# A quarter of block 4's gates through ScalarE and GpSimd while the route runs

## The chip, the core and the metric

The kernel runs on one core of a Trainium2 chip. A core has five engines, each with its own queue of instructions, executed in order: TensorE (PE in the profile; PEld is its loading of weights), VectorE (DVE), ScalarE (ACT), GpSimd (POOL) and SyncE (SP, which here only issues DMAs). They meet through semaphores. TensorE writes its results to PSUM, a memory of eight banks of 128 x 512 float32 numbers; the others work between PSUM and SBUF, except that in this kernel GpSimd only works on SBUF. The metric is the time of one execution on the device, in microseconds, and less is better.

## What is computed

Four blocks run one after the other over 2048 tokens of width 128: two attention blocks with their feed-forward parts, a third attention block, and block 4, a mixture of 64 small experts. Only block 4 is touched:

```
router_scores = softmax(xt @ Wr + br)
fs = _grouped_routing_scores(router_scores)      # sort each expert's scores, groups of 64, keep the best
up = jnp.einsum('td,edh->teh', xt, Wup) + bup
gate = jnp.einsum('td,edh->teh', xt, Wgate) + bgate
h = silu(up) * gate * fs[:, :, None]
out = jnp.einsum('teh,ehd->td', h, Wdown) + fs @ bdown
```

The 64 experts have 32 hidden features each, so the ups are a matrix of 2048 features by 2048 tokens, and the gates another. The routing sorts the scores of every expert over its tokens and keeps the best groups; it needs no up and no gate, and these need no routing until the product with `fs`.

## The kernel before

**The route.** The function `route` is the backbone: sorting passes on VectorE (`sort_pass`: one max and one min per pass over two halves of an SBUF tile, L1504 and L1505), then a search for the threshold by five counts over 2048 numbers (L1875), then small instructions that exchange sums with TensorE (L1906 to L1942), a scan (L1958) and the mask. After it the rows are multiplied by the weights and TensorE does the down projection (`stage_d`).

**The experts.** Between these instructions the class `Experts` places the up and gate work. The 2048 x 2048 plane is cut into 32 units of 256 features by 512 tokens, each of two halves (128 x 512), so there are 64 halves. `up` issues one matmul on TensorE and a Silu with bias on ScalarE out of PSUM into the unit's rows `hid` (L1650). `feed` issues gate matmuls ahead and keeps three (four when the ups are used up) in the list `ready`; an up is issued first where its half still lacks it. `fill(n)` takes up to n of the waiting gates: for each, VectorE adds the bias and multiplies the PSUM tile into `hid` in one instruction (L1664), then one further up and one further gate matmul are issued. All up and gate matmuls stand on one line, L1641, in `matmul`. PSUM gives them four banks.

**The order.** `stage_d` runs under a manual schedule: on TensorE, ScalarE, VectorE and GpSimd the instructions keep the order in which the program writes them. A fill is written after one sorting pass or more, so VectorE's order is pass, pass, gate, pass, pass, gate. Near the end come `fill(3)` at L1861, L1894, L1909, L1927 and L1940, placed where VectorE would wait for TensorE, and `fill(64)` at L1957, which takes what is left.

**Other names.** `c_xn` is a tag of one SBUF buffer of 128 x 512 float32: block 3 uses it at its start, and `route` at its end for `r_chosen`. The halves of the sorted keys are exchanged by two DMAs (L1830 on SyncE, L1831 on ScalarE's queue) before L1837. GpSimd has two memsets in the route and just after it, L1956 and L1692. L1858 and L1859 transpose the group sums on TensorE and copy them on ScalarE for the first count.

Of the kernel before, what the change touches and what calls it, by code (L numbers as in the profile page):

```python
# [22 lines left out]
F32 = mybir.dt.float32  # L23
BF16 = mybir.dt.bfloat16
AF = mybir.ActivationFunctionType
ALU = mybir.AluOpType
AX = mybir.AxisListType

P = 128
# [481 lines left out]
def add_tiles(k, x, ps):  # L511

    k.nc.vector.tensor_tensor(x, x, ps.rearrange("p (i d) -> p i d", d=D), ALU.add)
# [498 lines left out]
class BlockC:  # L1012
# [391 lines left out]
    def gate(self, b, j):  # L1404

        k, nc, st = self.k, self.k.nc, self.st[b]
        at, n = self.GROUPS[j]
        local, remote = st["local", j][:, :n], st["remote", j][:, :n]
        gs = self.p2.tile([P, 2, 64], F32, tag="gs", name=k.name("gs"))
        g = gs[:, 0, : n * 16]  # L1410
        l3 = local.rearrange("p m (h d) -> p (m h) d", d=8)
        pws = []
        last = (b, j) == (NB - 1, 2)
        eng = nc.vector if last else nc.gpsimd

        def products():
            for a, wn in ((local, "c_gl"), (remote, "c_gr")):
                pw = self.p2.tile([P, 64, 8], F32, tag="pw", name=k.name("pw"))[:, : n * 16]
                eng.tensor_tensor(
                    pw, a.rearrange("p m (h d) -> p (m h) d", d=8),  # L1420
                    k.row(wn)[:, None, :].to_broadcast([P, n * 16, 8]), ALU.mult,
                )
                pws.append(pw)
            if not last:
                eng.tensor_tensor(local, local, remote, ALU.subtract)

        def sums():
            for i in range(2):
                nc.vector.tensor_reduce(gs[:, i, : n * 16], pws[i], AX.X, ALU.add)
            nc.vector.tensor_tensor(g, g, gs[:, 1, : n * 16], ALU.add)  # L1430
            if last:
                tanh()
                eng.tensor_tensor(local, local, remote, ALU.subtract)

        def tanh():
            nc.scalar.activation(g, g, AF.Tanh, scale=0.5)

        def mix():
            if not last:
                tanh()  # L1440
            eng.tensor_scalar(g, g, 0.5, 0.5, ALU.mult, ALU.add)
            eng.tensor_tensor(l3, l3, g[:, :, None].to_broadcast([P, n * 16, 8]), ALU.mult)
            eng.tensor_tensor(local, local, remote, ALU.add)

        mT = self.p1.tile([P, 512], F32, tag="mT", name=k.name("mT"))

        def features():
            ps = k.mm()
            for i in range(n):
                nc.tensor.transpose(ps[:, i * P : (i + 1) * P], local[:, i, :], k.ident)  # L1450
            nc.scalar.copy(mT[:, : n * P], ps[:, : n * P])

        def out():
            ps = k.mm()
            for i in range(n):
                nc.tensor.matmul(
                    ps[:, i * D : (i + 1) * D], mT[:, i * P : (i + 1) * P], k.c_out,
                    start=True, stop=True,
                )
            add_tiles(k, k.xo[:, b * MT + at : b * MT + at + n], ps[:, : n * D])  # L1460
            self.front.tiles(self.pipe, b, at, n)

        beats = (0, 0, 1, 1, 1) if last else (1, 2, 1, 3, 2)
        steps = ((False, products), (False, sums), (False, mix), (True, features), (True, out))
        if last:
            products()
            sums()
            beats, steps = beats[2:], steps[2:]
        self.pipe.chain(*((n, *step) for n, step in zip(beats, steps)))
# [134 lines left out]
class Experts:  # L1604
# [50 lines left out]
    def feed(self):  # L1655

        while self.gates and len(self.ready) < (3 if self.ups else 4):
            unit, e = self.gates.pop(0)
            while (unit, e) in self.ups:
                self.up()  # L1660
            ps, hd = self.matmul(unit, e, self.k.d_gate), self.hid[unit][:, e, :]
            bias = self.k.col("d_bgate", unit[2] + 8 * e)
            self.ready.append(
                lambda ps=ps, hd=hd, bias=bias: self.k.nc.vector.scalar_tensor_tensor(  # L1664
                    hd, ps, bias, hd, ALU.add, ALU.mult
                )
            )

    def fill(self, n=1):

        for _ in range(n):
            if self.ready:
                self.ready.pop(0)()
                self.up()
                self.feed()


def stage_d(k, out, front, ex):
# [104 lines left out]


def route(k, p1, front, fill):


# [23 lines left out]
    for n, f in enumerate(front.todo):  # L1811
        f()
        left = len(front.todo) - n
        if left in (24, 13, 11):
            next(first)
        elif left == 6:
            next(second)
        fill(n % 2 if left < 10 else n % 3 > 0)
# [6 lines left out]
    while j >= 1:  # L1825
        sort_pass(k, za, zb, 1024, j, j == 512)
        fill()
        za, zb = zb, za
        j //= 2
# [384 lines left out]
```

## Time and profile before

| what | value |
|---|---|
| median of 3 runs | 1298.76 us (1298.31 to 1298.89) |
| profiled execution | 1301.14 us, of which the span of instructions is 1299.4 us |
| mean granted TensorE clock | 0.963 |
| busy: PE, PEld, DVE, ACT, POOL | 1155.7, 741.2, 869.4, 645.1, 477.8 us |
| L1664, gates on VectorE | 64 instructions, 747 ns each, 1085.3 to 1205.2 us |
| L1650, Silu on ScalarE | 64 instructions, 686 ns each |
| L1641, ups and gates on TensorE | 256 records (two for a matmul), 1052.9 to 1204.3 us |
| VectorE's waits for L1641 ahead of L1664 | 5.9 us in 7 waits |
| GpSimd in 1085 to 1205 us | two memsets, 1.09 us |

How to read it: the span runs from the first to the last instruction of one profiled execution, and the runs without a profile are the ones that the median is taken from. Busy shares are averages over stages with very different limits, so for a change in one stage the rows of that stage count: its busy times, its waits, and the chain of work that ended last, followed back from the last instruction. A row of a timeline has the start, the duration, the engine, the line, the operation, what it writes and reads, and in brackets how long the engine was idle ahead of it and who released it.

### The profile page before, as it was taken

How to read it: one execution, taken by the hardware profiler on the slowest of the kernel's cores; microseconds unless marked ns; L12 is line 12 of the kernel's file. 1: busy time of each engine (PE TensorE's matmuls, PEld its weight loads, DVE VectorE, ACT ScalarE, POOL GpSimd, SP SyncE). 2: the span in 40 equal slices, each digit the busy share in tenths (PEclk: the TensorE clock that was granted, in tenths of full speed). 3: DMA queues.
4: the chain of work that ended last, by engine and by line, in shares of the span. 5: the costliest groups of instructions: out<-in, count | busy, mean ns of one | idle time of the engine just before them, and what ended most of it. 6: DMA issues, size and time to landing. Idle time of an engine off the chain costs nothing.

```text
span 1299.4 us, 23474 instructions
## 1 busy us (share of the span) xinstructions
PE 1155.7 (89%) x9441; PEld 741.2 (57%) x9441; DVE 869.4 (67%) x1794; ACT 645.1 (50%) x1212; POOL 477.8 (37%) x556
## 2 busy tenths in 40 slices
PE   5899999998588999999999787989999967898798
PEld 3566666665356666666656544655555532343698
DVE  5566666565477776776776535566568969998763
ACT  5455455454345665665665545666756743342000
POOL 1523333232488776676686342221231210000000
PEclk9899999999799999999999988989988988999899
DMA  9000000000010000010100030000000000000000
GB/s 294 2 1 1 1 1 1 2 1 1 17 26 22 23 22 18 22 26 18 26 22 18 5 109 9 1 2 2 1 2 1 2 1 1 0 17 0 25 17 17
DMA packets 19841, 25.18 MB, mean 19 GB/s; under 512 B 2762, under 2 KB 13716, under 8 KB 19476
## 3 DMA queue, kind: packets, MB, share of 16 engines
q1 hardware_dynamic: 19076, 23.02, 6.3%
q8 instruction: 75, 1.23, 0.4%
q10 hardware_dynamic: 656, 0.66, 0.2%
q14 instruction: 34, 0.28, 0.1%
HBM read 13.32 MB, written 1.05 MB: 11 GB/s over the span
## 4 chain that ended last, share of the span: by engine, by line
PE 43%; DVE 19%; ACT 7%; issue 3%; POOL 2%; DVEq 0%; POOLq 0%; ACTq 0%
PE big L1641 6%; PE mm L1716 5%; PE bank L947 4%; PE s L714 3%; PE s L822 3%; PE s L1250 2%; PE bank L867 2%; PE s L1246 2%; PE tr L1287 2%; DVE nm L1255 2%; PE bank L964 2%; DVE rinv L736 2%; DVE rinv L737 1%; PE mm L1298 1%; PE s L817 1%
## 5 line engine op out<-in xcount | busy, mean ns | idle before, releaser
L1255 DVE TENSOR_REDUCE nm<-s 128x4 f32<-128x1024 f32 (+1 forms) x64 | 71.0, 1152 | 59.9 <-PE s L1250 59.7
L761 POOL TENSOR_TENSOR t<-raw,tab 128x512 f32<-128x512 f32 x64 | 79.7, 1265 | 77.7 <-DVE raw L752 77.7
L377 DVE TENSOR_REDUCE nm<-s 128x1 f32<-128x1024 f32 x64 | 75.1, 1216 | 48.7 <-PE s L371 48.7
L1288 ACT COPY pT<-tr 128x512 f32<-128x512 f32 x120 | 70.0, 597 | 73.0 <-PE tr L1287 72.8
L1650 ACT ACTIVATE hid<-big,cols 128x512 f32<-128x512 f32 x62 | 41.9, 686 | 75.8 <-PE big L1641 75.7
L1287 PE MATMUL tr<-ident,pr 128*128 128x128 f32 x480 | 77.2, 284 | 2.6 <-ACT pT L1288 2.3
L768 POOL TENSOR_TENSOR raw<-raw,tab 128x1024 f32<-128x1024 f32 x32 | 75.4, 2358 | 2.4
L1641 PE MATMUL big<-xTd,d_gate 128*128 128x512 f32 x128 | 66.1, 610 | 11.2 <-ACT hid L1650 7.5
L723 ACT ACTIVATE sq<-s 128x1024 f32<-128x1024 f32 x32 | 32.8, 1024 | 85.7 <-PE s L714 85.7
L1641 PE MATMUL big<-xTd,d_up 128*128 128x512 f32 x128 | 70.5, 642 | 5.3 <-DVE hid L1664 3.2
L383 ACT ACTIVATE pr<-s,nm 128x1024 f32<-128x1024 f32 x64 | 71.0, 1120 | 8.3 <-DVE nm L377 8.2
L775 POOL TENSOR_TENSOR raw<-raw,t 128x1024 f32<-128x1024 f32 x31 | 73.2, 2361 | 1.7
L394 PEld LDWEIGHTS bank<-ident,pr 128*128 128x128 f32 x512 | 56.6, 142 | 30.0 <-issue 22.5
L406 PE MATMUL bank<-pT,v 128*64 128x128 f32 x1024 | 71.0, 282 | 0.7 <-DVE pT L399 0.2
L397 ACT COPY pT<-bank 128x512 f32<-128x512 f32 x64 | 34.9, 587 | 68.7 <-PE bank L394 68.7
L406 PEld LDWEIGHTS bank<-pT,v 128*64 128x64 f32 x1024 | 55.8, 138 | 22.5 <-issue 11.1
L1287 PEld LDWEIGHTS tr<-ident,pr 128*128 128x128 f32 x480 | 54.7, 144 | 21.0 <-issue 11.6
L371 PE MATMUL s<-kk,q 64*128 64x512 f32 x256 | 65.1, 619 | 0.6 <-ACT pr L383 0.5
L394 PE MATMUL bank<-ident,pr 128*128 128x128 f32 x512 | 65.7, 277 | 0.0
L714 PE MATMUL s<-b_wqkv,hT 128*128 128x512 f32 x128 | 64.0, 623 | 1.3 <-ACT hT L682 1.3
L1716 PEld LDWEIGHTS mm<-d_down,hid 128*128 128x128 f32 x496 | 60.4, 194 | 5.7 <-DVE xo L1747 1.9
L1716 PE MATMUL mm<-d_down,hid 128*128 128x128 f32 x496 | 61.1, 278 | 1.3 <-DVE xo L1747 1.3
(363 smaller groups left out, 2816.6 us busy)
## 6 DMA issues: line engine op xcount, KB each, us to landing
vs<-v SPq DMA_DIRECT2D x60, 130.0 KB, 2.2
b_wqkv<-in_L_ffn_wqkv_dram SPq DMA_DIRECT2D x2, 768.0 KB, 9.3
b_tab<-in_c_xpos_dram SPq DMA_DIRECT2D x1, 1024.0 KB, 8.0
d_up<-in_L_ffn_Wup_dram SPq DMA_DIRECT2D x1, 1024.0 KB, 5.4
d_gate<-in_L_ffn_Wgate_dram SPq DMA_DIRECT2D x1, 1024.0 KB, 7.3
out_dram<-xo SPq DMA_DIRECT2D x3, 256.0 KB, 2.3
rows<-in_rows_dram SPq DMA_DIRECT2D x1, 760.0 KB, 6.5
b_w<-in_L_ffn_w_dram SPq DMA_DIRECT2D x2, 341.0 KB, 8.1
```

The source lines that it names most:

```text
L377: nc.vector.tensor_reduce(t["nm"][h], t["s"][h], AX.X, ALU.max, negate=True)
L383: nc.scalar.activation(t["pr", h], t["s"][h], AF.Exp, bias=t["nm"][h], accum_out=st["sums"][:, h, qt % 4 : qt % 4 + 1],)
L394: nc.tensor.transpose(ps[:, i * P : (i + 1) * P], t["pr", h][:, at : at + P], k.ident)
L406: nc.tensor.matmul(t["u"][h * 64 : h * 64 + 64, :P], v[:, kb, h * 64 : h * 64 + 64], t["pT"][:, h, kb], start=(kb == 0), stop=(kb == MT - 1),)
L714: nc.tensor.matmul(qk[:, cut], lhsT, k.b_wqkv[:, l, cut], start=True, stop=True)
L761: nc.gpsimd.tensor_tensor(t2[:, :, :, a : a + 32], r4[:, :, :, z : z + 32], self.tabs[l][1][:, m, :, None, a : a + 32].to_broadcast([P, 2, ...
L768: nc.gpsimd.tensor_tensor(r4, r4, self.tabs[l][0][:, m, :, None, :].to_broadcast([P, 2, 8, 64]), ALU.mult)
L775: eng.tensor_tensor(flat, flat, t["t2"].rearrange("p j h d -> p (j h d)"), ALU.add)
L1255: nc.vector.tensor_reduce(nm[h], view[h], AX.X, ALU.max, negate=True)
L1287: nc.tensor.transpose(ps[:, c * P : (c + 1) * P], pr[:, c, t * P : (t + 1) * P], k.ident)
L1641: self.k.nc.tensor.matmul(ps, weights[:, rows], self.xT[:, cut], start=True, stop=True)
L1716: nc.tensor.matmul(sums[part][:, cols], hid[tp, h, c][:, e, cols], k.d_down[:, c + 8 * e, :], start=start and e == 0, stop=False,)
```

## The change

In `feed` the entry of `ready` becomes a tuple with a flag. The flag is set where, after the half is taken from the list, the number of gates left gives 1 modulo 4. In `fill` a flagged half goes to ScalarE, which writes gate plus bias to a temporary in SBUF (tag `c_xn`), and GpSimd multiplies the temporary into `hid`; the others go to VectorE as before. A flagged half does not count against n.

```diff
             ps, hd = self.matmul(unit, e, self.k.d_gate), self.hid[unit][:, e, :]
             bias = self.k.col("d_bgate", unit[2] + 8 * e)
-            self.ready.append(
-                lambda ps=ps, hd=hd, bias=bias: self.k.nc.vector.scalar_tensor_tensor(
-                    hd, ps, bias, hd, ALU.add, ALU.mult
-                )
-            )
+            self.ready.append((len(self.gates) % 4 == 1, ps, hd, bias))
+
+    def gate(self, aside, ps, hd, bias):
+        nc, k = self.k.nc, self.k
+        if aside:
+            t = k.wpool.tile([P, 512], F32, tag="c_xn", name=k.name("aside"))
+            nc.scalar.activation(t, ps, AF.Identity, bias=bias)
+            nc.gpsimd.tensor_tensor(hd, hd, t, ALU.mult)
+        else:
+            nc.vector.scalar_tensor_tensor(hd, ps, bias, hd, ALU.add, ALU.mult)
 
     def fill(self, n=1):
 
-        for _ in range(n):
-            if self.ready:
-                self.ready.pop(0)()
-                self.up()
-                self.feed()
+
+        while n and self.ready:
+            now = self.ready.pop(0)
+            self.gate(*now)
+            self.up()
+            self.feed()
+            n -= not now[0]
```

## The prediction

> **What bounds the kernel now.** I began with the busy times of each engine in stretches of the route (sort and selection of block 4, 1085 to 1205 us of the span), where all changed instructions run. Each engine's column is busy us and the number of instructions.
>
> ```profile
> 1125.00:1142.00 17.00, 16.22 (x35) 5.85 (x36) 17.00 (x29) 5.50 (x8) 0.00 (x0) 1.00 0.00 0
> 1142.00:1161.00 19.00, 18.71 (x55) 8.44 (x54) 18.38 (x27) 9.22 (x15) 0.00 (x0) 1.00 0.13 28
> 1161.00:1180.00 19.00, 14.80 (x34) 5.52 (x32) 18.14 (x42) 6.32 (x10) 1.09 (x2) 1.00 0.00 0
> ```
>
> The order is TensorE matmul, its weight loads, VectorE, ScalarE, GpSimd. VectorE is full (17.00 of 17), ScalarE a third to half busy, GpSimd empty. But TensorE is nearly full beside it (18.71 of 19). Then the chain of waits:
>
> ```profile
> 1126.72 32.17 PE big L1641 x70
> ...
> 1176.19 2.35 DVE r_zab L1875 x2
> 1178.55 0.66 DVE hid L1664
> ```
>
> For 32 us it runs through the matmuls of L1641, and only then through VectorE. The two are level: relief of VectorE pays until TensorE is the later one. Third, TensorE's matmuls in order of time (a float32 matmul is two records, so each row is one half's up or gate):
>
> ```profile
> 1129.48 1.13 PE L1641 MATMUL big<-xTd,d_up 128*128 128x512 f32 x2
> 1130.44 1.02 PE L1641 MATMUL big<-xTd,d_gate 128*128 128x512 f32 x2
> 1131.38 1.13 PE L1641 MATMUL big<-xTd,d_up 128*128 128x512 f32 x2
> ...
> 1149.10 1.02 PE L1641 MATMUL big<-xTd,d_gate 128*128 128x512 f32 x2
> 1149.96 1.02 PE L1641 MATMUL big<-xTd,d_up 128*128 128x512 f32 x2
> 1150.82 1.02 PE L1641 MATMUL big<-xTd,d_gate 128*128 128x512 f32 x2
> ```
>
> At its fastest a matmul starts each 0.858 us (1149.10, 1149.96, 1150.82), so an up and a gate, a pair, take 1.715 us. Around 1130 a pair takes 1.90: the up waits until the Silu before it has freed its PSUM bank.
>
> **What the change does, in counts.** The condition picks halves 2, 6, ... 62 (counted from 0): 16 of 64. A fill now pays its n in VectorE gates and does passing halves on top. So 48 VectorE gates remain, the same fills are met in the same order, and the gates are used up at the 48th, the first of the fill(3) at L1909 (1182.52 us now). Up to there each fill brings 4/3 of a pair.
>
> **Part 1, what VectorE loses.** A gate takes 747 ns, but the next instruction starts 0.66 us after its start, so 16 gates are 10.6 us. They all go at the end: after gate 48 (1183.2) the fills are empty until the scan L1958 (1205.20). Those 22.0 us are 16 gates (10.6), waits of 5.6 like the one below, and 5.8 of the selection's own small instructions.
>
> ```profile
> 1183.97 0.75 DVE L1664 SCALAR_TENSOR_TENSOR hid<-big,cols,hid 128x512 f32<-128x512 f32 x1 [0.71 <-PE big L1641]
> ```
>
> What is late next are the hand-overs to TensorE at L1906, L1926 and L1936, which the gates cover now: a small matmul takes about 0.3 us and each hand-over 0.05 to 0.1, some 0.9 together with what gate 48 and L1938 still cover. The stretch becomes 5.8 + 0.9 = 6.7: **-15.3 us**.
>
> **Part 2, what TensorE must do earlier.** VectorE gate 39, the last before the first big count L1875 (1161.85), is now half 51. From 1086.11, when halves 0 to 3 have their gates and the ups are ahead, TensorE must issue 48 gates and 48 ups: 96 x 0.858 = 82.4; its first two start slow (1.87 and 1.52 instead of 0.86): +1.7; the 16 transposes of L1858 stand before half 51 in its order: +2.3. That is 1172.5; with the matmul's tail 0.16, the gate 0.66 and two small instructions 0.35, L1875 starts at 1173.7: **+11.8 us**, if TensorE never stops. It did stop between 1086 and 1159: 70 calls are 61.7 us with the slow start, of 72.6. Most of these 10.9 us are gaps behind VectorE, which the denser order fills; for those early on, while three halves are waiting and TensorE may not run ahead, I keep **+2** (bounds 0 and 5). In the five rounds of L1875 (3.59 us each) 4/3 pair costs 2.3, so nothing is added.
>
> **Part 3, ScalarE.** The Identity with bias out of PSUM has a row, L1147, and its product on GpSimd has L316, of the same shape:
>
> ```profile
> L1147 ACT ACTIVATE qT<-mm,cols x4: 687/687/738, 766.0 to 842.5; 128x512 f32<-128x512 f32 x4
> L316 POOL TENSOR_TENSOR kk<-kt,a_rot x8: 1260/1272/1277, 18.6 to 227.1; 128x512 f32<-128x512 f32 x8
> ```
>
> 16 x 0.69 = 11 us lie in idle ScalarE time (1.0 to 1.2 us ahead of each Silu). Behind an Identity on ScalarE stand the next Silu, and behind that the next up; the half was computed three pairs before, so nothing waits. If that cover were gone, a Silu would be 0.69 late. No table load is added: L1147 ran between exponentials without one. But where the bank freed by ScalarE is reused at once a pair takes 1.90, as at 1130; half of 48 pairs x 0.185 is 4.4 (bounds 0 and 8.9), most of it inside stops already counted: **+1**.
>
> **Part 4, GpSimd.** 16 x 1.27 us on an idle engine; the temporary has one buffer, but a side half comes only each fourth. Behind the last product on its queue stand the memsets L1956 (0.95) and L1692; the scan that needs the first comes several us later. The half swap's DMA from ScalarE's queue (L1831) stands behind Silus as now, and the gates of the fills between cover its 3 us.
>
> Here a rule speaks against the change. The Trainium skill, GPSIMD Engine Reference, section Key points, says that GpSimd shares its SBUF interfaces with VectorE and contends with VectorE instructions that have two SBUF inputs. All sort passes have two; the gate itself, with PSUM as one input, has one. The rule has no price. The trace has, where products of block 3 meet early passes:
>
> ```profile
> 1039.99 0.79 POOL L1443 TENSOR_TENSOR local<-local,remote 128x256 f32<-128x256 f32 x1
> ...
> 1040.23 0.84 DVE L1504 TENSOR_TENSOR r_zab<-r_zab 128x256 f32<-128x256 f32 x1
> ...
> 1040.99 0.41 DVE L1505 TENSOR_TENSOR r_zab<-r_zab 128x256 f32<-128x256 f32 x1
> ```
>
> The pass that starts inside the product takes 0.84 instead of the 0.41 of its twin: it is held until GpSimd is done (1040.78) and ends 0.29 later. A pass already running is not disturbed. So a 1.27 us product holds VectorE by 1.27, less what is left of the running pass (0.2 to 0.3), less 0.14: about 0.85. Of 16 products 12 (halves 2 to 46) lie among passes: between 0 (all fall on gates and waits) and 12 x 0.98 = 11.8. The row gives 0.85, some fall on a gate: 8 us held. The first seven products come while VectorE is level with TensorE and delay both; later ones fall into VectorE's waits for gates. I count less than half: **+3.3**. Without the rule the sum would be lower by this.
>
> **Sum.** -15.3 + 11.8 + 2 + 1 + 3.3 = **+2.8 us**. The profiled execution took 1301.14 (span 1299.4 and 1.7 around it), so it would take 1303.9; on the median of the runs shown, 1298.76, it is **1301.6 us**. A measurement of this kernel can tell about 0.2% (2.6 us) from no change.
>
> **Rivals.**
> - TensorE keeps its fastest pace and the holds fall into waits. For it: 1.715 per pair held from 1146 to 1158 and wherever VectorE waits. Against it: the row of L1504. Then 11.8 - 15.3 = -3.5: **1295.3**, faster. It decides if stops, bank waits and holds together stay under 3.5. VectorE alone (-15.3 and no delay) would be 1283, which Part 2 excludes.
> - The holds stay uncovered: 8 and the early 2 on the path, +6.5 in sum: **1305.3**. For it: early on VectorE has no slack. Against: later it waits for gates.
> - Banks: each pair at 1.90, 8.9 us, with holds hidden beneath: +5.4 to +6.4, **1304.7**. For it: the gaps at 1130. Against: from 1146 they are gone as soon as VectorE waits.
> - The change doesn't do what it says, because nothing is set aside or a table is loaded for each Identity (32 x 1.28 = 41 us): the rows of L1147 exclude the latter.
>
> **Chances.** The forecast's own case, 1298.8 to 1304.3: 0.50; fast rival 0.21; holds 0.16; banks 0.12; the last 0.01. Faster by over 0.2% (under 1296.2) takes nearly all of the fast rival: 0.19. The forecast's case divides about its middle, just past 1301.4: with the two slow rivals slower is 0.53, the same 0.28. The range leaves out a tenth each side: from 1294.5 (the fast rival and a little of unseen gain) to 1307.
>
> **What would show it.** 48 rows of L1664, 16 of Identity near 0.69 us and 16 products near 1.27; the first L1875 some 15 to 18 us later than 1161.85, the scan L1958 some 1 to 5 us later than 1205.20; passes of L1504 and L1505 with maxima above 1 us and about 8 us held in sum; VectorE's waits for L1641 up from 5.9 to near 10 us, and before L1875 now. I am wrong if L1875 starts before 1172, if the passes keep their means (290, 430 and 685 ns), or if a pair takes over 1.9 us where VectorE waits.

## The result, and the profile after

The changed kernel took 1303.2 us (median of 20 runs, 1301.57 to 1306.76), the kernel before, beside it on the same chip, 1299.95 us (20 runs, 1298.31 to 1304.18). The ratio is 1.0027, 95% interval 1.0019 to 1.0034: 3.5 us slower (2.5 to 4.4). The forecast was 2.8 us slower.

The profiled execution took 1301.58 us, with a span of 1299.8. It came into the route earlier than the one of before: L1578, one VectorE pass ahead of the first gates and alike in all kernels here, starts at 1075.20 in place of 1078.69. Over all profiles of this study that point lies between 1075.20 and 1081.41, so every stretch below is counted from L1578 and not from the start of the span. Line numbers behind the change are 7 or 8 higher: the gate is L1672, Identity L1669, product L1670, the counts L1882, the scan L1965.

| stretch, us | before | after | difference | forecast |
|---|---|---|---|---|
| L1578 to the first count | 83.16 | 99.92 | +16.8 | +18.1 |
| first count to the scan | 43.35 | 29.50 | -13.9 | -15.3 |
| scan to the end of the span | 94.2 | 95.2 | +1.0 | 0 |

First the busy times by stretches of the route in the profile after, to be laid beside those of before (the columns are TensorE, its weight loads, VectorE, ScalarE, GpSimd, each busy us and instructions, then TensorE's granted clock):

```profile
1125.00:1142.00 17.00, 16.88 (x39) 6.97 (x38) 16.80 (x25) 7.78 (x12) 4.13 (x3) 1.00 0.01 1
1142.00:1161.00 19.00, 19.00 (x45) 8.36 (x44) 14.71 (x21) 9.87 (x17) 2.54 (x2) 1.00 0.13 28
1161.00:1180.00 19.00, 18.68 (x55) 8.78 (x54) 14.00 (x23) 10.69 (x18) 4.43 (x3) 1.00 0.00 0
1180.00:1205.00 25.00, 12.60 (x31) 5.51 (x29) 21.91 (x62) 1.47 (x3) 4.83 (x5) 0.76 0.00 1
```

The last of these stretches, from 1180 to 1205, looked like this in the kernel before:

```profile
1180.00:1205.00 25.00, 23.73 (x65) 11.08 (x64) 19.08 (x48) 5.50 (x8) 0.00 (x0) 1.00 0.00 1
```

TensorE has become the full engine before the counts (19.00 of 19), and VectorE, full before, now has nearly a quarter free (14.71 of 19). In the last stretch it is the other way round: TensorE works half of the time (12.60 of 25), and its clock falls to 0.76 on the mean, where it had been 1.00. The chain of waits of the same profile (start, us, what) says where one takes over from the other:

```profile
1125.14 1.64 DVE r_zab L1504
1126.77 0.60 DVE r_zab L1505
1127.38 0.67 DVE hid L1672
1128.09 41.76 PE big L1641 x96
1169.85 0.45 PE tr L1865 x4
...
1172.10 1.73 PE big L1641 x4
1173.93 0.75 DVE hid L1672
1175.12 2.35 DVE r_zab L1882 x2
```

Up to 1127 it is made of VectorE's own instructions, then of 96 records of TensorE without a break, the transposes, and the two matmuls of half 51, which stand behind them. The first count (the chain's last row) waits for that half's gate. VectorE's timeline has the same gate, with 4.01 us of idle time ahead of it, and another of the waits that it now has in the sort:

```profile
1151.08 0.75 DVE L1672 SCALAR_TENSOR_TENSOR hid<-big,cols,hid 128x512 f32<-128x512 f32 x1 [2.75 <-PE big L1641]
1173.93 0.75 DVE L1672 SCALAR_TENSOR_TENSOR hid<-big,cols,hid 128x512 f32<-128x512 f32 x1 [4.01 <-PE big L1641]
```

The added instructions (minimum, median and maximum in ns; the sixteenth product, of 1267 ns, has a row of its own, since the last rows of `hid` lie in another buffer), and a product among VectorE's passes in the timeline:

```profile
L1669 ACT ACTIVATE aside<-big,cols x16: 679/681/689, 1085.3 to 1196.0; 128x512 f32<-128x512 f32 x16
L1670 POOL TENSOR_TENSOR hid<-hid,aside x15: 1263/1270/1892, 1086.1 to 1184.6; 128x512 f32<-128x512 f32 x15
```

```profile
1094.49 1.27 POOL L1670 TENSOR_TENSOR hid<-hid,aside 128x512 f32<-128x512 f32 x1 [7.16 <-ACT aside L1669]
1094.60 1.31 DVE L1504 TENSOR_TENSOR r_zab<-r_zab 128x128 f32<-128x128 f32 x1
...
1095.83 0.28 DVE L1505 TENSOR_TENSOR r_zab<-r_zab 128x128 f32<-128x128 f32 x1
```

The pass of 128 numbers, 0.29 us as a rule, takes 1.31 and ends 0.15 after the product (1095.76). Eleven VectorE instructions are prolonged so, 8.25 us in all over what their line and shape take as a rule: ten in the sort and one small instruction of the count rounds. In the kernel before none is. No gate of L1672 is among them, and none of the long counts L1882, which read one tensor from SBUF.

### The profile page after: what moved, and what is told of

It is laid out like the page before. It is cut to its first block, busy times and chain, and to the rows that moved or that the text cites. A ratio compares the mean times of both kernels' runs of the same rounds, so it can differ in the third digit from the quotient of the medians.

```text
span 1299.8 us, 23422 instructions
## 1 busy us (share of the span) xinstructions
PE 1144.8 (88%) x9381; PEld 744.6 (57%) x9441; DVE 866.8 (67%) x1778; ACT 655.3 (50%) x1228; POOL 501.0 (39%) x572
## 3 DMA queue, kind: packets, MB, share of 16 engines
HBM read 13.32 MB, written 1.05 MB: 11 GB/s over the span
## 4 chain that ended last, share of the span: by engine, by line
PE 40%; DVE 20%; ACT 7%; issue 4%; POOL 3%; DVEq 0%; POOLq 0%; ACTq 0%
PE mm L1723 5%; PE big L1641 4%; PE bank L947 4%; PE s L714 3%; PE s L822 3%; PE s L1250 2%; PE bank L867 2%; DVE r_zab L1504 2%; PE tr L1287 2%; DVE nm L1255 2%; PE s L1246 2%; DVE rinv L736 2%; DVE r_zab L1505 2%; PE bank L964 1%; DVE rinv L737 1%
## 5 line engine op out<-in xcount | busy, mean ns | idle before, releaser
L761 POOL TENSOR_TENSOR t<-raw,tab 128x512 f32<-128x512 f32 x64 | 79.7, 1267 | 77.1 <-DVE raw L752 73.1
L1641 PE MATMUL big<-xTd,d_gate 128*128 128x512 f32 x128 | 67.6, 620 | 8.0 <-DVE r_above L1887 4.3
L1641 PE MATMUL big<-xTd,d_up 128*128 128x512 f32 x128 | 70.6, 643 | 4.5 <-DVE hid L1672 4.2
```

Of the source, the lines that this page charges most:

```text
L761: nc.gpsimd.tensor_tensor(t2[:, :, :, a : a + 32], r4[:, :, :, z : z + 32], self.tabs[l][1][:, m, :, None, a : a + 32].to_broadcast([P, 2, ...
L1641: self.k.nc.tensor.matmul(ps, weights[:, rows], self.xT[:, cut], start=True, stop=True)
```

## The experiments

All stretches are from one profile each and counted as above; ratios are to the kernel before on the same chip, with 95% intervals, from 5 (five late) to 22 runs of each kernel. "Held" is the time by which VectorE's instructions exceed the median of their line and shape. "Clock back" is how long after the scan's start the trace's clock record shows TensorE at full clock again.

| kernel | L1578 to count | count to scan | scan to end | clock back | held, us | ratio |
|---|---|---|---|---|---|---|
| before | 83.16 | 43.35 | 94.2 | 13.8 | 0 | 1 |
| changed | 99.92 | 29.50 | 95.2 | 15.8 | 8.25 | 1.0027 (1.0019 to 1.0034) |
| no product | 96.91 | 29.17 | 95.2 | 15.8 | 0 | 1.0002 (0.9993 to 1.0010) |
| one-input product | 97.17 | 30.05 | 94.5 | 14.4 | 1.85 | 0.9998 (0.9989 to 1.0006) |
| counted | 86.78 | 47.65 | 94.5 | 14.1 | 10.14 | 1.0051 (1.0039 to 1.0064) |
| five late | 83.14 | 39.48 | 95.0 | 15.6 | 0 | 0.9967 (0.9955 to 0.9979) |
| before + 16 two-input | 86.63 | 44.04 | 94.8 | 14.6 | 4.72 | 1.0023 (1.0016 to 1.0030) |
| before + 16 one-input | 84.35 | 45.32 | 94.3 | 14.1 | 1.95 | 1.0022 (1.0012 to 1.0031) |
| the same, second profile | 84.34 | 45.31 | 94.4 | 14.1 | 1.96 | one run |
| before + 10 one-input | 84.33 | 43.35 | 93.6 | 12.7 | 1.69 | 1.0006 (0.9998 to 1.0015) |
| changed, TensorE kept busy | 100.03 | 28.77 | 94.7 | 14.9 | 7.98 | 1.0017 (1.0008 to 1.0027) |
| five late + two early | 84.64 | 36.45 | 95.2 | 15.8 | 1.82 | 0.9951 (0.9933 to 0.9969) |

The profiles differ in one thing that no edit made. Ahead of the first gates TensorE's full clock came back 10.6 us after L1578 in six of them (before, the three with one-input passes added, TensorE kept busy, five late + two early) and 11.9 to 12.2 us after it in the other six. The first stretch doesn't show it (before 83.16, five late 83.14), but where the clock falls later, a difference between a profile of the one group and one of the other can in part be this.

### What do the holds cost?

**No product.**

```diff
             nc.scalar.activation(t, ps, AF.Identity, bias=bias)
-            nc.gpsimd.tensor_tensor(hd, hd, t, ALU.mult)
```

> As the changed kernel, with GpSimd's 16 products left out, so that the Silu of 16 halves goes into the down product without its gate; ScalarE's Identity pass, the fills and TensorE's work stay. Theory (part 4 of the prediction): the 11 prolonged VectorE passes (8.25 us together) go, some 3.3 us of them were on the path, the first count starts 2 to 4 us earlier counted from the first gate, and the time falls to 1299 to 1300.5, a ratio to the kernel before of 0.999 to 1.0005. Rival A (TensorE's own pace is the whole of it, the holds lie in its shadow): first count and ratio as with the product, 1.002 to 1.003. Rival B (the holds are on the path in full): 8 us less, a ratio near 0.996.

The ratio fell from 1.0027 to 1.0002: 3.2 us, as the theory had it; rival A (nothing) is outside the interval, and so is rival B (0.996). The first count came 3.0 us earlier. So of 8.25 held us some 3 were on the path. The chains say why not all. Without the product the chain runs through TensorE from the first gates to the transposes:

```profile
1084.45 84.24 PE big L1641 x188
```

So VectorE has some time to spare there. The 5.3 us held before 1128 use that up first, and only the rest makes VectorE the later engine; the 2.9 behind 1128 lie in the shadow of TensorE.

**One SBUF input.**

```diff
-            nc.gpsimd.tensor_tensor(hd, hd, t, ALU.mult)
+            nc.gpsimd.tensor_scalar(hd, t, 1.0, None, ALU.mult)
```

> As the changed kernel, with GpSimd's product replaced by a pass with one SBUF input of the same 512 elements (the set-aside gate times 1.0 written into the row, so the Silu factor of these 16 halves is left out). Theory (holds come from two SBUF inputs on both engines): no prolonged VectorE pass, the ratio as without a GpSimd pass, 0.999 to 1.0005. Rival (any GpSimd pass of that length holds VectorE): 8 us prolonged as before, ratio 1.002 to 1.003.

The time is that of the theory. "No prolonged VectorE pass" was not right: six are longer, by 0.15 to 0.41 us. The timeline of this kernel shows a different thing from the row above:

```profile
1125.84 1.57 POOL L1670 TENSOR_SCALAR hid<-aside 128x512 f32<-128x512 f32 x1 [5.92 <-ACT aside L1669]
1126.10 0.98 DVE L1504 TENSOR_TENSOR r_zab<-r_zab 128x512 f32<-128x512 f32 x1
...
1127.00 0.68 DVE L1505 TENSOR_TENSOR r_zab<-r_zab 128x512 f32<-128x512 f32 x1
```

The pass (0.68 as a rule) ends at 1127.08, inside GpSimd's instruction (until 1127.41), and the next one runs beside it at its own speed. It is delayed, not held to the end.

**The two-input pass alone.** The kernel before, with a pass on GpSimd that nobody reads behind each fourth gate; the diff is against the changed kernel, from which it was made.

```diff
+        nc.vector.scalar_tensor_tensor(hd, ps, bias, hd, ALU.add, ALU.mult)
         if aside:
             t = k.wpool.tile([P, 512], F32, tag="c_xn", name=k.name("aside"))
-            nc.scalar.activation(t, ps, AF.Identity, bias=bias)
-            nc.gpsimd.tensor_tensor(hd, hd, t, ALU.mult)
-        else:
-            nc.vector.scalar_tensor_tensor(hd, ps, bias, hd, ALU.add, ALU.mult)
+            nc.gpsimd.tensor_tensor(t, hd, hd, ALU.mult)
...
-            n -= not now[0]
+            n -= 1
```

> The kernel before (all 64 gates on VectorE, one counted per gate) with one thing added: after each fourth gate, 16 times, GpSimd multiplies the finished row by itself into the scratch tile, two SBUF inputs, 128x512, and nothing reads the product. Theory (the hold is a price of its own, paid in full wherever VectorE is the bound, which it is from the sort to the first count in the kernel before): 10 to 12 passes prolonged by 1.07 each, first count 9 to 12 us later counted from L1578, in all +9 to +13, ratio 1.007 to 1.010. Rival A (the holds mostly lie beside waits that VectorE has anyway): +2 to +4, ratio 1.0015 to 1.003. Rival B (the aside's Identity and the bank it keeps are the price, not the product): ratio 1.000.

The size was that of rival A, 1.0023, but not its reason. VectorE has no wait at all between L1578 and the first count, so nothing hides a hold: 4.03 us were held there, and the first count came 3.47 later (the kernel before has 0.8 us of waits in that stretch, which can have taken up the rest). What was wrong is how many holds there are and how long: seven instead of 10 to 12, and 0.18 to 0.84 instead of 1.07. The added product starts as a gate ends, when the pass behind the gate is already running and only the one after that can be caught, and it takes 1.04 us where it is undisturbed, not 1.27:

```profile
1096.37 0.28 DVE L1505 TENSOR_TENSOR r_zab<-r_zab 128x128 f32<-128x128 f32 x1
1096.39 1.15 POOL L1670 TENSOR_TENSOR aside<-hid 128x512 f32<-128x512 f32 x1 [8.04 <-DVE hid L1667]
1096.68 1.01 DVE L1504 TENSOR_TENSOR r_zab<-r_zab 128x128 f32<-128x128 f32 x1
```

Rival B is excluded: there is no Identity here, and the loss is there.

### Is TensorE's pace the other half?

**Counted.** A half set aside counts against n.

```diff
-            n -= not now[0]
+            n -= 1
```

> As the changed kernel, but a half set aside counts as one of a fill's gates, so that pairs are taken at the pace of the kernel before and 22 us of gates are left to the end. Theory (part 2: the pace of 4/3 pairs makes TensorE late by about 12 us, the holds by 3): in the sort 10 to 11 gates fewer on VectorE (-7 us) stand against 8 us of holds, so the first count comes within 2 us of the kernel before, 13 to 15 us ahead of the changed kernel; the tail loses the 3 or 4 gates that are set aside in it (-2.5 us); in all 1297 to 1300, ratio 0.998 to 1.000. Rival (the holds alone make the change's loss, whatever the pace): the first count 8 us later than before and a ratio of 1.003 or more.

A clear miss: 1.0051, slower than the changed kernel. TensorE's lateness went as expected (the first count only 3.6 us later than before, not 16.8), but with it went the shadow. This kernel's VectorE waits 0.9 us before the first count, much as in the kernel before (0.8), and its passes are held nearly to the full:

```profile
1125.33 1.45 POOL L1670 TENSOR_TENSOR hid<-hid,aside 128x512 f32<-128x512 f32 x1 [8.98 <-ACT aside L1669]
...
1125.57 1.76 DVE L1505 TENSOR_TENSOR r_zab<-r_zab 128x512 f32<-128x512 f32 x1
```

Eight such holds of 1.02 to 1.08, 8.5 us, stand against nine gates of 0.66, 5.9 us. So in the sort **setting a half aside costs VectorE more than the gate that it saves**. (That difference is 2.6; about 1 us of the 3.6 is not accounted for.) The stretch from the count to the scan did not become shorter by 2.5 but longer by 4.3. Two small instructions of the rounds are held there, by 1.06 and 0.54. Then TensorE sets the pace, so gates taken off VectorE bring nothing, and its clock had fallen in the count rounds: VectorE waits 1.98 and 1.93 us where it had waited 0 and 0.71. How the 4.3 divide between holds and clock was not separated. In this kernel's busy times (TensorE first, its clock third from the end):

```profile
1180.00:1186.00 6.00, 3.45 (x4) 1.40 (x5) 4.50 (x11) 0.69 (x1) 0.00 (x0) 0.62 0.00 0
```

### What does TensorE's clock cost?

**TensorE kept busy in the changed kernel.**

```diff
         nc.vector.tensor_scalar(junk, every, piv, None, ALU.is_gt, ALU.add, accum_out=above)
         fill()
+        ps = k.tr()
+        for _ in range(2):
+            nc.tensor.matmul(ps, k.ident, every[:, :512], start=True, stop=True)
```

> The changed kernel with two added 128x512 matmuls (identity times the table of sums, never read) behind the pair of each of the five count rounds, 5 x 1.72 us, so that TensorE doesn't idle there. Theory (the clock that fell to half in the rounds cost the gates and transposes behind them some 2 us, and the first down matmuls about 1): granted clock 1.00 from 1180 to about 1195, first count to scan 27.5 to 28.5 in place of 29.5, in all 1 to 2 us faster than the changed kernel, ratio 1.001 to 1.002. Rival (the fall of the clock lies beside VectorE's own work): as the changed kernel, 1.0027; or, if the added matmuls come in the gates' way, above it.

The clock stayed at 1.00 from 1182 to 1200, and the count-to-scan stretch lost 0.73 us, less than the 1 to 2 expected. The ratio, 1.0017, is where the theory put it, but its interval overlaps that of the changed kernel. This is consistent with a cost of about 1 us, not proof of it.

**One-input passes added to the kernel before.** The diff is that of the two-input kernel with `nc.gpsimd.tensor_scalar(t, hd, 1.0, None, ALU.mult)` as the added pass.

> As the kernel before with 16 added GpSimd passes, but each with one SBUF input (the row times 1.0 into the scratch tile). Theory (only two inputs on both engines hold): passes prolonged by at most 0.4 each and 2 us together, ratio 1.000 to 1.0015. Rival (any GpSimd pass holds): as with two inputs.

Held were 1.95 us, as expected, but the ratio was 1.0022, above the theory's 1.000 to 1.0015 (its interval, from 1.0012, reaches into it). In the profile 1.2 us were lost before the first count and 2.0 behind it, where one small instruction was prolonged by 0.27. The busy times of this kernel have the clock at half there:

```profile
1177.29:1180.70 3.41, 1.54 (x4) 0.30 (x2) 3.31 (x10) 0.69 (x1) 0.39 (x1) 1.00 0.00 0
1180.70:1184.11 3.41, 3.41 (x6) 1.62 (x6) 2.56 (x9) 0.69 (x1) 1.30 (x1) 0.50 0.00 0
```

Two kernels followed: this one's second profile, and one with only the ten passes of the sort (`len(self.gates) % 4 == 1 and len(self.gates) > 24` as the flag).

> The kernel before with all 16 added one-input passes, a second profile of the same kernel. If the clock's fall at the end of the count rounds belongs to this kernel, it shows again near 1180 to 1186 and first count to scan is near 45.3; if it was that one execution's, the clock is 1.00 there and the stretch 43.5 to 44.

> As the kernel before with added GpSimd passes of one SBUF input, but none of them in the count rounds or behind them (those with more than 24 gates left only, 10 passes in the sort). Theory (with all 16, 1.2 us were lost in the sort to passes prolonged by 0.3 to 0.4, and the rest behind the first count, where the one profile showed the clock at 0.72 for 6 us): first count 1 to 1.5 us later than in the kernel before, first count to scan 43.3 to 43.8, ratio 1.0005 to 1.0015. Rival (the passes in the sort cost the whole): ratio 1.0022 again.

The second profile repeats the first to 0.01 us (84.34 and 45.31; the clock at half from 1182.1 to 1185.5). With the passes kept out of the rounds the clock does not fall, the stretch is 43.35 as in the kernel before, and the ratio is 1.0006. So in these two profiles a prolongation of 0.27 us on VectorE, in rounds that leave TensorE idle for half the time, was followed by one window at half clock and cost 2 us with it. That it does so in every execution isn't shown: the profiles compared here all have the clock back 10.6 us after L1578. In the two-input kernel (12.1) the same small instruction was held by 0.69, and the clock stayed. The intervals of 1.0022 and 1.0006 overlap.

### A version that beats both

**Five late.** Only the halves that come up in the count rounds are set aside, where VectorE's long instruction has one SBUF input and TensorE has time to spare.

```diff
-            self.ready.append((len(self.gates) % 4 == 1, ps, hd, bias))
+            self.ready.append((len(self.gates) in (24, 22, 20, 18, 16), ps, hd, bias))
```

> As the changed kernel, but only five halves are set aside, those that come up in the five count rounds (with 24, 22, 20, 18 and 16 gates left), where VectorE's long passes have one SBUF input and TensorE has time to spare; 59 gates stay on VectorE. Theory: nothing is prolonged, the first count starts where it does in the kernel before, each round brings one more pair without VectorE time, five gates fewer are left for the end (5 x 0.66 to 0.75 = 3.3 to 3.7 us less, tail 22 to 18.5), ratio 0.9970 to 0.9980. Rival (TensorE or the banks set the rounds, or the products hold the rounds' small passes): 1.000 or above.

0.9967, from five runs, is 4.3 us faster than the kernel before (2.7 to 5.8), a little more than the theory's 0.9970 to 0.9980. Nothing is held, the first count comes at 83.14 as before (83.16), and the stretch to the scan is 3.9 us shorter. In its timeline a product and a count run side by side, the count at its usual 2.35:

```profile
1165.44 2.35 DVE L1875 TENSOR_SCALAR_CACHE_REDUCE r_zab<-r_every,r_piv 128x2048 f32<-128x2048 f32 x1
```

```profile
1166.23 2.35 DVE L1882 TENSOR_SCALAR_CACHE_REDUCE r_zab<-r_every,r_piv 128x2048 f32<-128x2048 f32 x1
```

```profile
1166.96 1.27 POOL L1670 TENSOR_TENSOR hid<-hid,aside 128x512 f32<-128x512 f32 x1 [2.15 <-ACT aside L1669]
```

The first row is a count of the kernel before, the second one of this kernel, the third the product that lies inside it.

**Five late and two early.** The flag is `len(self.gates) in (54, 46, 22, 20, 18, 16, 14)`.

> The version with five halves set aside in the count rounds, with two more set aside in the first half of the sort (with 54 and 46 gates left), where TensorE has 4.6 us to spare. Theory: each of the two is held once for 1.07 us on VectorE and takes one pair of 1.72 us out of the end, which TensorE bounds: 2 x 0.65 = 1.3 us faster than the version with five, ratio 0.9955 to 0.9965. Rival (TensorE is late at the first count, or the end isn't TensorE's): 1 to 2 us slower than the version with five, 0.998.

0.9951. From L1578 to the scan it is 1.5 us ahead of five late, as the theory had it (1.3), with two holds of 0.76 and 1.07. The intervals of the two ratios overlap, so by the times alone the two versions aren't told apart; both beat the kernel before.

## Why the prediction was right

**What bounds the kernel.** VectorE and TensorE nearly level, so that relief of the one makes the other late: shown by the chain after, which changes over at 1128. "Level" was too kind to VectorE: in the sort of the kernel before it waits 0.8 us in 83.

**Part 1, the end: -15.3 expected, -13.9 measured.** The gates were used up at the 48th, as counted. The term for exposed hand-overs was too small, since it was taken at full clock: gate 48 waits 1.05 for cold matmuls, L1936 0.62 and L1949 0.56. With TensorE kept busy the stretch is -14.6.

**Part 2, TensorE: +11.8, with 2 for stops, and part 3's 1 for banks; 14.8 expected, 13.75 measured** (the kernel without the product, 96.91 less 83.16). The mechanism was the right one, half 51 behind the transposes. Stops and banks cost about 2 together (13.75 less 11.8), not 3. The chain of that kernel agrees: its 188 records are 94 matmuls, which at 0.858 with the forecast's slow start make 82.3 us, and they took 84.24.

**Part 3, ScalarE: nothing on the path.** Identity took 0.68 us each. Without part 4 the forecast's sum is -0.5 us; the kernel without the product measured +0.3 (-0.9 to +1.3).

**Part 4, the holds: 8 us held and 3.3 on the path expected; 8.25 and 3.2 measured.** The rule of two SBUF inputs, which had no price, was the one to weigh, and the price read from a row of block 3 was good: 0.85 a pass, where ten were held by 0.42 to 1.07, 0.79 on the mean. That the later ones fall into VectorE's waits was argued before and is borne out: where TensorE isn't late (the counted kernel) eight holds cost more than nine gates bring. But "less than half" of the 8 us was a judgement and not a sum, so that 3.3 came so near to 3.2 has luck in it.

**Not in the sum: +1.0 behind the scan.** TensorE's full clock comes back 15.8 us after the scan in place of 13.8, which would lengthen the first down matmuls. Over the twelve profiles the last stretch runs with that figure, from 93.6 us at 12.7 to 95.2 at 15.8; no run changes the clock alone. Part of it is chance: two profiles whose rounds keep the clock at full, before and the one with ten added passes, differ by 0.6. How much of it the changed kernel pays on the mean was not measured.

**What would show it.** Sum of the profiled differences: 16.8 - 13.9 + 1.0 = 3.9; the times say 3.5. That the forecast's 2.8 is so close is in part luck: the three stretches were off by -1.3, +1.4 and +1.0, and the first two cancel. From L1578 the first count is 16.8 later and the scan 2.9, both as written. Taken from the start of the span they are +13.3 and -0.6 and miss, because this execution was 3.5 us ahead when it came into the route: landmarks belong to a nearby anchor. VectorE's waits for L1641 rose from 5.9 to 10.1, and 9.1 of them now lie before the first count.

**The rivals.** The fast one (-3.5) asked for hidden holds and no stops. The holds were not hidden, and even without them the kernel is level with the one before: 2 us went into TensorE's stops, 1.1 into the colder end, 1.0 behind the scan. The second rival, uncovered holds, is nearer to the counted kernel, in which TensorE isn't late. The bank rival needs a pair of 1.90 throughout; the chain has 96 records in 41.76 us, which is 1.74 a pair.

## What to carry to other kernels

Work moved from VectorE to GpSimd is paid by what VectorE runs beside it: among passes with two SBUF inputs each 1.27 us product held a pass by up to 1.1, more than the 0.66 that it saved; beside instructions with one SBUF input it was free. Where two engines are nearly level, move the work where the other has spare time: five halves in the right place gained 4.3 us, sixteen spread evenly lost 3.5. Stretches that leave TensorE idle for half the time need a look at the clock: in two profiles here a quarter of a microsecond there went with a loss of two.

## What the hardware showed that was not expected

**The clock falls after windows that are not idle.** In the trace's clock records here, every stretch at half clock that ends within the span lasts a multiple of 3.41 us (3.4, 6.8, 10.2, 13.7, 17.1, 20.5, 27.3). The Trainium skill, TensorE: Matmul & The Clock Gate, Part 1, has a free-running window of that length and lists the half clock as the state after an idle window. The windows that preceded a fall in the count rounds were not idle. Cut on that grid, the kernel with sixteen two-input passes, where the clock stayed:

```profile
1176.47:1179.89 3.42, 1.56 (x4) 0.38 (x2) 3.38 (x5) 0.69 (x1) 0.71 (x1) 1.00 0.00 0
1179.89:1183.30 3.41, 2.97 (x8) 1.46 (x9) 3.29 (x13) 0.69 (x1) 0.11 (x1) 1.00 0.00 0
```

and the changed kernel, where it fell:

```profile
1186.29:1189.70 3.41, 1.46 (x4) 0.49 (x3) 3.34 (x7) 0.00 (x0) 0.00 (x0) 1.00 0.00 0
1189.70:1193.11 3.41, 1.27 (x2) 0.00 (x0) 3.31 (x7) 0.00 (x0) 0.00 (x0) 0.50 0.00 0
```

TensorE (first column) was busy for 1.46 of 3.41 us before a fall here, 1.54 in the kernel with one-input passes, and 1.27 in the counted one; 1.56 and 1.81 did not bring one. That looks like an edge a little below half of a window, but the same traces speak against it. In five late the clock fell just behind a window with 1.81 us:

```profile
1193.12:1196.54 3.42, 1.81 (x7) 0.79 (x5) 3.35 (x9) 0.00 (x0) 0.00 (x0) 1.00 0.02 5
1196.54:1199.90 3.36, 0.00 (x0) 0.00 (x0) 3.36 (x4) 0.00 (x0) 0.00 (x0) 0.50 0.00 0
```

In block 3 of the changed kernel it fell behind one with 2.62 (954.21 to 957.62). So a busy time as the profile gives it, with the ends of matmuls modelled, doesn't decide it alone; what does stays open.

**Two ways of being held.** A two-input product on GpSimd holds a two-input VectorE pass that starts inside it to its own end (1.31 us in place of 0.29, above). A one-input pass on GpSimd, 1.49 us long, delays it by 0.15 to 0.42 and runs on beside it. GpSimd is held in its turn: where a VectorE pass runs as it starts, its product takes up to 1.89 in place of 1.27, and its one-input pass in the kernel before with sixteen added up to 2.83 in place of 1.49.
